# Four blocks of an FP4 layer, the scatters and the gathers of a mixture: another place in the order of a woven kernel

## The chip, the cores and the metric

The kernel runs on one core of a Trainium2 chip. A core has five engines that run side by side and wait for each other by semaphores: TensorE (PE in the profile; its weight loads are shown as PEld), VectorE (DVE), ScalarE (ACT), GpSimd (POOL) and SyncE (SP), which issues most of the transfers. Each engine takes its instructions in the order in which they stand in its own queue. The metric is the device time of one execution in microseconds, the median of the runs shown; less is better. Numbers such as L455 are lines of the kernel before the change.

## What is computed

The reference is a chain of twelve residual layers on `x`, 4 sequences of 1024 tokens with 128 features: FP4 feed-forward, softmax attention with a recurrent and a GELU part, the same FP4 feed-forward again; then twice a mixture of experts (L1) around a softmax attention, twice another mixture with a shared expert (L2) around a linear attention, twice a ternary feed-forward (L3) around another linear attention. The parts that this change touches:

```python
def fp4_quant_dequant(x):          # blocks of 16 along the last dimension
    xb = x.reshape(shape[:-1] + (shape[-1] // BLOCK, BLOCK))
    scale = jnp.maximum(jnp.max(jnp.abs(xb), axis=-1, keepdims=True) / 6.0, 1e-12)
    idx = jnp.searchsorted(_MID, jnp.abs(xb / scale))
    return (_GRID[idx] * jnp.sign(xb / scale) * scale).reshape(shape)

# layers 0 and 2:  x = x + 0.5 * _L0_ffn_ref(_layernorm(x), ...)
gate, y = fp4_linear(x, w_gate), fp4_linear(x, w_up)        # 128 -> 352
return fp4_linear(silu(gate) * y, w_down)                   # 352 -> 128

# layers 3 and 5 (6 and 8: logits softmaxed over the top two, silu(h), a shared expert)
probs = softmax(x @ gate_w.T); w, idx = top_k(probs, 2); w = w / sum(w)
for gup, dn, ce in experts:                                 # 8 experts
    g, u = split(x @ gup.T, 2); acc += ce * (silu(g) * u @ dn.T)
```

## The kernel before, in words

`x` stays in SBUF as 8 blocks of 512 tokens. `version[blk]` counts how many layers a block has been through; `need(blk, n)` lets a generator idle until the block has reached layer n.

**Woven generators.** Every layer is a Python generator that issues some instructions and yields. `run` goes through `ORDER`, a list written by hand of turns and of the layers that begin with each. A turn is a layer, or (layer, half) for the two halves (four blocks each) of a mixture. After each step of the turn, `tick` gives one step to the task at the head of each lane in `LANES`: fetch (the gathers of a half that is done), ends, front (layernorm, router, places and scatters of a mixture), alone (the shared expert), linear, ahead. The order in which instructions are issued, on all engines, follows from this weaving; a compile-time pass then orders each engine's queue by this priority and by what its estimate says is ready.

**FP4 layers** (turns 0 and 2). `l0_ffn` weaves `l0_block` over all 8 blocks, two at a time, a new one after 12 steps at the earliest. A block: layernorm; `fp4` quantises it (maximum, scale, reciprocal on DVE, a product on POOL at L447, four DVE steps L451 to L454, another product on POOL at L455); transposes; then for each of two pairs of token tiles: gate and up products (L505) into a `big` buffer of PSUM (two of them), SiLU on ACT, product on DVE (L509), `fp4` again on 128x704, transposes, down products (L521). The down products of both pairs go into one bank `out`, held over the block, and one DVE step at L527 adds half of it to `x`. That is 22 steps a block.

**Mixtures** (layers 3, 5, 6, 8). `front` takes two blocks at a time: for each, layernorm into `xn` (three buffers), transposes, router logits; then `router` and `placed` find the rows of each token at its two experts (L1099 is the cast to integer rows); then 16 scatters (L1426, an indirect transfer that POOL issues, two for each of 8 token tiles) put the normed tokens into `rows_in`. After four blocks the half's `which` (the expert of each tile) is set, and `tiles` can begin: 20 tiles of 256 rows, each with weights (L1487) and rows (L1488) loaded through SP's queue two tiles ahead, transposed (L1505), multiplied (L1546, L1555, L1532) and stored to `rows_out` (L1518). A branch at L1593 runs up to three more tiles where the data need them. `back` then gathers the results (32 gathers a half, L1625, POOL again) and adds them into `x` (L1612). Where the next half's `which` is not set when its turn comes, `run` only ticks and sets `waits_for` to the layer; `back` of that layer takes no new block meanwhile.

**Pace.** `paced` is the last DVE instruction of a few busy loops (the maxima of attention at L649, the experts' products); scatters and gathers get a semaphore wait on it (`pace`), and the second part of `layernorm` is queued behind it on DVE, so that side tasks spread over the work they stand beside.

The order around the change:

```python
ORDER = (
    ((0,), 0), ((1,), 1), (("mixtures", 2, 3), 2), ((), (3, 0)), ((4,), (3, 1)), ((5,), 4), ((), (5, 0)),
    ((6,), (5, 1)), ((), (6, 0)), ((7, 8), (6, 1)), ((), (8, 0)), ((9,), (8, 1)), (("-mixtures", 10), 9), ((11,), 11),
)
```

Of the kernel before, what the change touches and what calls it, by code (L numbers as in the profile page):

```python
# [16 lines left out]
AF = mybir.ActivationFunctionType  # L17
# [155 lines left out]
LANES = ("fetch", "ends", "front", "alone", "linear", "ahead")  # L173
# [21 lines left out]
class _Kernel:  # L195
# [6 lines left out]
    def __init__(self, ctx, tc, ins, out):  # L202
        self.tc, self.nc, self.ins, self.out = tc, tc.nc, ins, out
        self.const = ctx.enter_context(tc.tile_pool(name="const", bufs=1))
        self.small = ctx.enter_context(tc.tile_pool(name="small", bufs=4))
        self.mix = ctx.enter_context(tc.tile_pool(name="mix", bufs=2))
        self.memory = ctx.enter_context(tc.tile_pool(name="memory", bufs=1, space=bass.MemoryType.DRAM))
        self.version = [0] * NBLK
        self.paced = None
        self.easy = False  # L210
        self.waits_for = None
# [137 lines left out]
    def layernorm(self, dst, src):  # L349
# [75 lines left out]
    def fp4(self, pool, src, p, n):  # L425
# [28 lines left out]
        v.scalar_tensor_tensor(y, e, -STEP, y, ALU.mult, ALU.add)  # L454
# [28 lines left out]
    def l0_ffn(self, k):  # L483
        pool, close = self.opened("l0f", "left")
        yield from woven((self.l0_block(pool, blk, k) for blk in range(NBLK)), 2, 12)
        close()

    def l0_block(self, pool, blk, k):
# [3 lines left out]
        yield from self.layernorm(xn, self.x[blk])  # L492
# [5 lines left out]
        out = self.acc()  # L498
        for pair in range(TPB // 2):
# [13 lines left out]
            for i in range(2):  # L513
                ps = self.transposed([hq[:, i * I0 + c * C0 : i * I0 + (c + 1) * C0] for c in range(4)])
                hqT = pool.tile([C0, 4, P], F32, tag="hqT", name="hqT", bufs=4)
                nc.scalar.copy(hqT.rearrange("p c t -> p (c t)"), ps[:C0, :])
                hqTs.append(hqT)
                yield
            for i in range(2):
                for c in range(4):  # L520
                    nc.tensor.matmul(  # L521
                        out[:, bass.ts(2 * pair + i, D)], lhsT=hqTs[i][:, c, :], rhs=self.wdT[:, c, :],
                        start=c == 0, stop=c == 3,
                    )
# [95 lines left out]
    def maxima(self, pool, n, qb, causal):  # L620
# [8 lines left out]
        for t in range(TPB):  # L629
            q = qb * TPB + t  # L630
            keys = (q + 1) * P if causal else S
            for c in range(0, keys, BLK):
                w = min(keys - c, BLK)
                diag = causal and c + w == keys
                for pair in range(2):
# [7 lines left out]
                    if diag:  # L643
# [5 lines left out]
                    self.paced = nc.vector.tensor_reduce(  # L649
                        to[:, pair::2, t], ps[:, :, :w], AX.X, ALU.max, negate=True  # L650
# [585 lines left out]
    def l3_ffn(self, k):  # L1236
# [22 lines left out]
        for two in range(0, NBLK, 2):  # L1259
            hs = []  # L1260
            for blk in (two, two + 1):
# [4 lines left out]
                for c in range(NC):  # L1266
                    ps = self.big()
                    for j, m in enumerate((w1, w2)):
                        nc.tensor.matmul(ps[:, j, :], lhsT=m[:, bass.ts(c, P)], rhs=xnT, start=True, stop=True)  # L1269
                    nc.scalar.activation(h[:, c, :], ps[:, 0, :], AF.Silu, scale=scale(0, c))  # L1270
                    nc.vector.scalar_tensor_tensor(  # L1271
                        h[:, c, :], ps[:, 1, :], scale(1, c), h[:, c, :], ALU.mult, ALU.mult
# [5 lines left out]
            for i0, m in ((2, h1), (3, h2)):  # L1278
                for z in range(2):
                    h = pool.tile([P, NC, BLK], F32, tag="h", name="h", bufs=4)  # L1280
                    for pair in range(NC // 2):
# [30 lines left out]
    def run(self):  # L1312
# [47 lines left out]
class _Mixture:  # L1360
# [27 lines left out]
    def front(self, half, first, blocks):  # L1388
# [28 lines left out]
        half.todo += blocks  # L1417
        if half.todo == HALF:
# [16 lines left out]
        if half.todo == HALF:  # L1435
# [3 lines left out]
    def twice_silu(self, h, x):  # L1439

        self.k.nc.scalar.activation(h, x, AF.Tanh, scale=0.5)  # L1441
        self.k.paced = self.k.nc.vector.scalar_tensor_tensor(h, h, 1.0, x, ALU.add, ALU.mult)
# [52 lines left out]
    def tiles(self, half, behind):  # L1495
# [43 lines left out]
        def products(j, w, xT, first=None, last=None):  # L1539

            nonlocal waiting
            for c in range(0, NC, many):
# [10 lines left out]
                else:  # L1553
                    nc.scalar.activation(h, ps[:, :many, :], AF.Silu)  # L1554
                    k.paced = nc.vector.tensor_tensor(h, h, ps[:, many:, :], ALU.mult)  # L1555
# [46 lines left out]
    def back(self, half):  # L1602
# [51 lines left out]
```

## Time and profile before

| what | us |
|---|---|
| median of 3 runs | 4490.01 (4486.51 to 4496.32) |
| the profiled execution | 4454.02 |
| its span, first to last instruction | 4452.3 |
| first FP4 layer, blocks done (L527) | 71 to 223 |
| attention of layer 1, last maxima | 1091; its tail ends at 1279 |
| second FP4 layer, blocks done | 1187, 1241, 1281, 1320, 1344, 1373, 1413, 1435 |
| scatters of blocks 0 and 1, of 2 and 3, of 4 to 7 | 1292 to 1316, 1372 to 1394, 1451 to 1525 |
| tiles of (3, 0), (3, 1) | 1442 to 1568, 1568 to 1753 |
| attention of layer 4 | to about 2661 |
| tiles of (5, 0), (5, 1) | 2661 to 2785, 2785 to 3002 |
| tiles of (6, 0), (6, 1) | 3009 to 3165, 3175 to 3354 |
| tiles of (8, 0), (8, 1) | 3417 to 3585, 3598 to 3711 |
| last layers (L3, linear attention, L3) | 3711 to 4452 |

The borders of the stages come from the times of a line's instructions. In the busy table a stretch is followed by the busy time of each engine with the number of its instructions, the granted TensorE clock as a share of full speed, the share of DMA engines busy and the gigabytes per second. In a timeline, a line is a run of like instructions: start, length, engine, line, operation, what it writes and reads, how many, and in brackets the idle time of the engine before it and what ended it. In a list of waits, the three numbers are the sum, the times and the longest.

### The profile page before, as it was taken

What the parts mean: (1) busy time and instruction counts of PE and PEld (TensorE: products, weight loads), DVE (VectorE), ACT (ScalarE), POOL (GpSimd) and SP (SyncE); (2) the same over time, 40 slices, a digit from 0 to 9 for tenths busy, and PEclk for the clock granted to TensorE, in tenths of its full rate; (3) what the DMA queues carried; (4) which work ended last, traced back from release to release, by engine and by line L of the source; (5) the groups of instructions that cost most, each with busy time, mean ns of one, the idle gap of its engine ahead of it and who ended that gap; (6) DMA issues with size and microseconds to landing.
All of it is one profiled execution on the core that took longest, in us unless ns stands there. A gap on an engine that the chain in (4) does not pass through costs nothing. (4 is left out here: it accounts for less than half of the span.)

```text
span 4452.3 us, 59962 instructions
## 1 busy us (share of the span) xinstructions
PE 3783.8 (85%) x21360; PEld 1963.3 (44%) x21360; DVE 2665.9 (60%) x6035; ACT 1704.7 (38%) x3066; POOL 1024.5 (23%) x1334
## 2 busy tenths in 40 slices
PE   4659999999665978899989999887795978999999
PEld 3513333333344865222222338665563654444444
DVE  8657878785777446788888854535574653223201
ACT  1216454545222222566656662222231322333322
POOL 5313323222244231202020101324324142000000
PEclk8759899999876999999999999998897989999999
DMA  2011101000001553101010005434422352000000
GB/s 103 1 47 46 37 21 39 21 29 7 1 10 37 184 166 101 44 28 39 28 64 27 30 15 188 134 117 130 136 90 72 110 155 75 1 0 0 5 5 10
DMA packets 140628, 261.74 MB, mean 59 GB/s; under 512 B 25803, under 2 KB 90187, under 8 KB 139683
## 3 DMA queue, kind: packets, MB, share of 16 engines
q1 hardware_dynamic: 123939, 224.23, 15.6%
q0 software_dynamic: 16384, 33.59, 2.5%
q8 instruction: 174, 2.85, 0.3%
q14 instruction: 131, 1.07, 0.1%
HBM read 197.31 MB, written 60.42 MB: 58 GB/s over the span
## 5 line engine op out<-in xcount | busy, mean ns | idle before, releaser
L827 ACT ACTIVATE es<-sc 128x512 f32<-128x512 f32 (+3 forms) x1792 | 892.2, 549 | 576.3 <-PE sc L820 572.8
L649 DVE TENSOR_REDUCE part<-big 128x2 f32<-128x1024 f32 (+3 forms) x768 | 877.0, 1154 | 178.2 <-PE big L639 119.5
L742 PE MATMUL acc<-es,va 128*32 128x256 f32 (+2 forms) x6144 | 566.9, 411 | 4.1 <-POOL es L830 3.4
L1546 PE MATMUL big<-xT,w 128*128 128x256 f32 x1968 | 514.3, 402 | 24.1 <-DMA w<-in_l2f_w 9.8
L639 PE MATMUL big<-most 64*128 64x512 bf16 (+3 forms) x1792 | 385.3, 368 | 93.0 <-DMA most<-pieces 58.0
L1285 PE MATMUL big<-h,l3f_w 128*128 128x512 f32 x1024 | 446.6, 593 | 5.3 <-DVE h L1271 2.3
L1546 PEld LDWEIGHTS big<-xT,w 128*128 128x128 f32 x1968 | 387.1, 202 | 103.5 <-issue 35.4
L815 PE MATMUL sc<-most 64*128 64x512 bf16 (+3 forms) x1792 | 394.8, 371 | 24.8 <-ACT es L827 11.6
L361 POOL TENSOR_TENSOR ln_rs<-ln_ve,neg_half 128x4 f32<-128x4 f32 x120 | 125.8, 1049 | 1158.1 <-DVE ln_ve L360 1133.7
L1625 POOL DMA_INDIRECT y<-rows_out,rows x256 | 246.9, 965 | 564.4 <-DVE h L1555 155.2
L820 PE MATMUL sc<-last 64*128 64x512 bf16 (+3 forms) x1792 | 376.5, 365 | 0.0
L1532 PE MATMUL acc<-h,w 128*128 128x256 f32 x1304 | 342.8, 394 | 24.1 <-DVE h L1555 16.0
L1426 POOL DMA_INDIRECT rows_in<-xn,rows x256 | 249.8, 976 | 473.7 <-DVE p_to L1114 91.2
L1285 PEld LDWEIGHTS big<-h,l3f_w 128*128 128x128 f32 x1024 | 191.9, 190 | 239.1 <-issue 230.1
L830 POOL TENSOR_SCALAR_AFFINE_SELECT es<-es 128x128 f32<-128x128 f32 x512 | 171.3, 345 | 526.5 <-ACT es L827 521.2
L1532 PEld LDWEIGHTS acc<-h,w 128*128 128x128 f32 x1304 | 241.1, 197 | 67.8 <-DVE h L1555 23.7
L742 PEld LDWEIGHTS acc<-es,va 128*32 128x32 f32 x6144 | 135.7, 109 | 297.7 <-issue 242.5
L815 PEld LDWEIGHTS <-most 64*128 64x128 bf16 x1792 | 94.3, 93 | 376.2 <-issue 353.1
L1554 ACT ACTIVATE h<-big 128x512 f32<-128x512 f32 x166 | 99.1, 597 | 402.5 <-PE big L1546 394.7
L1441 ACT ACTIVATE h<-big 128x1024 f32<-128x1024 f32 x112 | 114.4, 1024 | 328.2 <-PE big L1546 238.3
L639 PEld LDWEIGHTS <-most 64*128 64x128 bf16 x1792 | 110.8, 95 | 236.1 <-issue 119.2
L1612 DVE SCALAR_TENSOR_TENSOR x<-y,weights,x 128x128 f32<-128x128 f32 x256 | 90.9, 361 | 207.0 <-DMA y<-rows_out,rows 206.0
(291 smaller groups left out, 5195.4 us busy)
## 6 DMA issues: line engine op xcount, KB each, us to landing
w<-in_l1f_w SPq DMA_DIRECT2D x86, 768.0 KB
w<-in_l2f_w SPq DMA_DIRECT2D x84, 512.0 KB
most<-pieces SPq DMA_DIRECT2D x512, 48.0 KB
xr<-rows_in SPq DMA_DIRECT2D x170, 128.0 KB
rows_out<-yr SPq DMA_DIRECT2D x163, 128.0 KB
pieces<-pieces SPq DMA_DIRECT2D x32, 384.0 KB
most<-pieces SPq DMA_DIRECT2D x256, 32.0 KB
rows_in<-zero SPq DMA_DIRECT2D x4, 1472.0 KB
```

The costliest lines, as they stand in the source:

```text
L639: nc.tensor.matmul(ps[:, j, :w], lhsT=of[:, 0, bass.ts(q, P)], rhs=of[:, 1, c : c + w], start=True, stop=not diag,)
L649: self.paced = nc.vector.tensor_reduce(to[:, pair::2, t], ps[:, :, :w], AX.X, ALU.max, negate=True)
L742: nc.tensor.matmul(out[0][32 * i : 32 * i + 32, lo:hi], lhsT=self.vas[b % 2][:, kc, (4 * g + i) * (HD + 1) :][:, :32], rhs=es[i][:, lo:hi] ...
L815: nc.tensor.matmul(ps[:, off:], lhsT=of[:, 1, keys], rhs=of[:, 0, queries], start=True, stop=False)
L820: nc.tensor.matmul(ps[:, off:], lhsT=of[:, 1 + pair, keys], rhs=of[:, 0, queries], start=False, stop=True,)
L827: nc.scalar.activation(es[i][:, off:], ps[:, off:], AF.Exp, scale=ISQ)
L830: nc.gpsimd.affine_select(out=block, in_=block, compare_op=ALU.is_ge, fill=0.0, base=0, pattern=[[1, P]], channel_multiplier=-1,)
L1285: nc.tensor.matmul(ps[:, j, :], lhsT=m[:, i * FF + (2 * pair + j) * P : i * FF + (2 * pair + j + 1) * P], rhs=hs[z][:, i, :], start=i == 0 ...
L1426: put = nc.gpsimd.indirect_dma_start(out=k.rows_in[half.h][:, :], out_offset=bass.IndirectOffsetOnAxis(ap=at, axis=0), in_=xns[t // TPB][: ...
L1532: nc.tensor.matmul(outs[j][:, :TT], lhsT=w[:, low + c * D :][:, :D], rhs=h, start=c == 0, stop=c == NC - 1)
L1546: nc.tensor.matmul(ps[:, i, :], lhsT=w[:, bass.ts(col, P)], rhs=xT, start=True, stop=True)
L1625: got = nc.gpsimd.indirect_dma_start(out=y, out_offset=None, in_=k.rows_out[half.h][:, :], in_offset=bass.IndirectOffsetOnAxis(ap=self.row ...
```

## The change

Layer 2 handles only its first four blocks in its turn and puts the other four, as one generator, into a new lane `ffn`; the main loop goes on to (3, 0) meanwhile. `l0_block` adds each pair of token tiles into `x` by itself, from a bank that it asks for only then (19 steps a block; layer 0 too). Scatters are a generator `put` in a new lane `puts`; `front` goes on without them, but holds at most three `xn` tiles (`held`). `waits_for` is now the half that the main loop waits for, and the gathers of the other half, whatever their layer, stop before each gather until that half begins. FP4's last DVE step, L3's products and L3's GELU now set the pace too; `pacer` is what transfers wait for, `paced` what layernorms are queued behind. FP4's own layernorm is not queued behind anything.

```diff
-LANES = ("fetch", "ends", "front", "alone", "linear", "ahead")
+LANES = ("fetch", "ends", "puts", "front", "alone", "linear", "ffn", "ahead")
...
-        with nullcontext() if self.paced is before else self.tc.issue_after(self.paced.ins):
+        with nullcontext() if in_turn or self.paced is before else self.tc.issue_after(self.paced.ins):
...
-        if self.paced is not None:
-            self.tc.add_manual_dep(transfer.ins, self.paced.ins.name, SYNC, reason="pace")
+        if self.pacer is not None:
+            self.tc.add_manual_dep(transfer.ins, self.pacer.ins.name, SYNC, reason="pace")
+
+    def passed(self, instruction):
+
+        self.paced = self.pacer = instruction
...
-        v.scalar_tensor_tensor(y, e, -STEP, y, ALU.mult, ALU.add)
+        self.passed(v.scalar_tensor_tensor(y, e, -STEP, y, ALU.mult, ALU.add))
...
-        yield from woven((self.l0_block(pool, blk, k) for blk in range(NBLK)), 2, 12)
-        close()
+
+        def blocks(first, last):
+            yield from woven((self.l0_block(pool, blk, k) for blk in range(first, last)), 2, 12)
+            if last == NBLK:
+                close()
+
+        if k == 0:
+            yield from blocks(0, NBLK)
+        else:
+            yield from blocks(0, HALF)
+            self.beside("ffn", blocks(HALF, NBLK))
...
-        yield from self.layernorm(xn, self.x[blk])
+        yield from self.layernorm(xn, self.x[blk], True)
...
-        out = self.acc()
+        x = self.x[blk].rearrange("p t d -> p (t d)")
         for pair in range(TPB // 2):
...
+            out = self.acc()
             for i in range(2):
                 for c in range(4):
                     nc.tensor.matmul(
-                        out[:, bass.ts(2 * pair + i, D)], lhsT=hqTs[i][:, c, :], rhs=self.wdT[:, c, :],
+                        out[:, bass.ts(i, D)], lhsT=hqTs[i][:, c, :], rhs=self.wdT[:, c, :],
                         start=c == 0, stop=c == 3,
                     )
-                yield
-        x = self.x[blk].rearrange("p t d -> p (t d)")
-        nc.vector.scalar_tensor_tensor(x, out, 0.5, x, ALU.mult, ALU.add)
-        self.version[blk] += 1
-        yield
+            these = x[:, bass.ts(pair, 2 * D)]
+            nc.vector.scalar_tensor_tensor(these, out[:, : 2 * D], 0.5, these, ALU.mult, ALU.add)
+            if pair == TPB // 2 - 1:
+                self.version[blk] += 1
+            yield
...
-                            nc.scalar.activation(h[:, c, :], ps[:, j, :], AF.Gelu, scale=scale(i0, c))
+                            self.pacer = nc.scalar.activation(h[:, c, :], ps[:, j, :], AF.Gelu, scale=scale(i0, c))
...
-                self.waits_for = turn[0]
+                self.waits_for = turn[1]
...
             yield from k.need(blk, self.number)
+            while k.held == max(TOGETHER) + 1:
+                yield
+            k.held += 1
...
-        for t in range(n):
+        k.beside("puts", self.put(half, first * TPB, xns, which))
+
+    def put(self, half, first, xns, which):
+
+        k, nc = self.k, self.k.nc
+        for t in range(len(xns) * TPB):
             for i in range(2):
-                at = self.rows[:, i, first * TPB + t : first * TPB + t + 1]
+                at = self.rows[:, i, first + t : first + t + 1]
                 put = nc.gpsimd.indirect_dma_start(
...
+            if t % TPB == TPB - 1:
+                k.held -= 1
+        if which is not None:
             k.apart(half.puts)
             half.which = which
...
-            while k.waits_for == self.number:
-                yield
             for t in range(blk * TPB, (blk + 1) * TPB):
                 for i in range(2):
+                    while k.waits_for == 1 - half.h:
+                        yield
                     y = k.mix.tile([P, D], F32, tag="y", name="y", bufs=4 * TPB)
```

The steps at L649, L1442 and L1555 that were assigned to `paced` are now passed to `passed`, and so is L1271. L1599, which sets `paced` back to what it was ahead of the branch, stays as it is.

More of the change, by code (lines that the diff above doesn't have):

```diff
@@ L209, in __init__ @@
         self.paced = None
+        self.pacer = None
         self.easy = False
+        self.held = 0
         self.waits_for = None
@@ L346, in clear_rows, with layernorm @@
                 )
-    def layernorm(self, dst, src):
+    def layernorm(self, dst, src, in_turn=False):
         nc = self.nc
@@ L648, in maxima @@
                     to = mx if one else part[:, c // BLK]
-                    self.paced = nc.vector.tensor_reduce(
-                        to[:, pair::2, t], ps[:, :, :w], AX.X, ALU.max, negate=True
+                    self.passed(
+                        nc.vector.tensor_reduce(
+                            to[:, pair::2, t], ps[:, :, :w], AX.X, ALU.max, negate=True
+                        )
                     )
@@ L1270, in l3_ffn @@
                     nc.scalar.activation(h[:, c, :], ps[:, 0, :], AF.Silu, scale=scale(0, c))
-                    nc.vector.scalar_tensor_tensor(
-                        h[:, c, :], ps[:, 1, :], scale(1, c), h[:, c, :], ALU.mult, ALU.mult
+                    self.passed(
+                        nc.vector.scalar_tensor_tensor(
+                            h[:, c, :], ps[:, 1, :], scale(1, c), h[:, c, :], ALU.mult, ALU.mult
+                        )
                     )
@@ L1417, in front @@
         half.todo += blocks
+        which = None
         if half.todo == HALF:
@@ L1434, in front @@
                     yield
-        if half.todo == HALF:
+            if t % TPB == TPB - 1:
+                k.held -= 1
+        if which is not None:
             k.apart(half.puts)
@@ L1441, in twice_silu @@
         self.k.nc.scalar.activation(h, x, AF.Tanh, scale=0.5)
-        self.k.paced = self.k.nc.vector.scalar_tensor_tensor(h, h, 1.0, x, ALU.add, ALU.mult)
+        self.k.passed(self.k.nc.vector.scalar_tensor_tensor(h, h, 1.0, x, ALU.add, ALU.mult))
     def alone(self, blk):
@@ L1554, in products @@
                     nc.scalar.activation(h, ps[:, :many, :], AF.Silu)
-                    k.paced = nc.vector.tensor_tensor(h, h, ps[:, many:, :], ALU.mult)
+                    k.passed(nc.vector.tensor_tensor(h, h, ps[:, many:, :], ALU.mult))
                 next(leaving, None)
```

## The prediction

> **What bounds the kernel now.** I read the page first, then the busy table cut at the stage borders, then the waits of PE and the timelines at the borders that hold a hole.
>
> ```profile
> span 4452.3 us, 59962 instructions
> PE 3783.8 (85%) x21360; PEld 1963.3 (44%) x21360; DVE 2665.9 (60%) x6035; ACT 1704.7 (38%) x3066; POOL 1024.5 (23%) x1334
> ...
> PE   4659999999665978899989999887795978999999
> ...
> PEclk8759899999876999999999999998897989999999
> ```
>
> PE is the busiest engine, and over most slices it is full, so time is won only where PE waits: slices 11 to 13 (1110 to 1440 us: the second FP4 layer), and slice 31 (3340 to 3450 us). There the granted clock falls too. The busy table (columns: stretch, length, PE, PEld, DVE, ACT, POOL, clock, DMA share, GB/s):
>
> ```profile
> 1110.00:1320.00 210.00, 144.10 (x608) 83.50 (x604) 155.07 (x431) 57.72 (x100) 77.99 (x73) 0.80 0.02 6
> 1320.00:1397.00 77.00, 35.95 (x171) 28.54 (x172) 54.92 (x176) 13.24 (x23) 38.85 (x34) 0.69 0.14 47
> 1397.00:1442.00 45.00, 29.88 (x147) 24.42 (x145) 32.40 (x107) 9.65 (x17) 15.91 (x14) 0.73 0.02 5
> 1442.00:1568.00 126.00, 122.38 (x599) 104.32 (x599) 60.59 (x185) 35.05 (x68) 37.88 (x40) 0.98 0.54 178
> 1568.00:1753.00 185.00, 150.13 (x652) 111.03 (x652) 97.45 (x200) 38.70 (x71) 36.00 (x36) 0.91 0.44 146
> ...
> 3165.00:3175.00 10.00, 0.76 (x5) 0.46 (x4) 1.12 (x3) 0.00 (x0) 4.84 (x5) 0.64 0.30 93
> ...
> 3354.00:3417.00 63.00, 12.97 (x39) 6.30 (x39) 24.52 (x123) 3.44 (x5) 41.90 (x43) 0.62 0.23 73
> 3417.00:3585.00 168.00, 152.13 (x695) 110.02 (x696) 112.27 (x349) 55.41 (x90) 36.65 (x38) 0.97 0.35 111
> 3585.00:3598.00 13.00, 3.54 (x17) 2.38 (x15) 2.73 (x5) 0.29 (x2) 7.44 (x8) 0.74 0.38 126
> ```
>
> The fourth row is (3, 0), the first half of the mixture behind the FP4 layer: PE 122 of 126 us busy. The rows above it are the FP4 layer, which runs on latency: no engine is full. What PE waits for there is the last step of a quantisation, on POOL:
>
> ```profile
> PE tr L377 <- POOL fp_y L455: 89.0, 16, 21.8
> ```
>
> The first instruction of (3, 0) comes without any wait just before it, behind FP4's and the router's matmuls in PE's own order:
>
> ```profile
> 1432.19 3.20 PE L521 MATMUL acc<-wdT,hqT 88*128 88x128 f32 x16
> ...
> 1442.14 1.11 PE L377 MATMUL tr<-ident,xr 128*128 128x128 f32 x4
> ```
>
> Its rows were there long before: the last scatter of its half ran at 1393 us. So (3, 0) could have begun at about 1400 us. The second hole, before (8, 0), is a wait for rows:
>
> ```profile
> 3387.30 0.95 POOL L1625 DMA_INDIRECT y<-rows_out,rows  x1 [0.30 <-issue]
> 3388.55 1.00 POOL L1426 DMA_INDIRECT rows_in<-xn,rows  x1 [0.30 <-issue]
> ...
> 3417.03 1.09 PE L377 MATMUL tr<-ident,xr 128*128 128x128 f32 x4 [14.45 <-DMA xr<-rows_in]
> ```
>
> The places of these scatters (L1099, the cast of the rows) were known at 3376 us in DVE's timeline; POOL was still in 22 gathers of the half before (3356 to 3388), and the scatters had to queue behind them.
>
> **The change, part by part.** A step of the woven generators I call a tick. A tile of an expert takes four, a half of 20 tiles 80; (8, 0) took 168 us, so a tick there is 2.1 us.
>
> *Four FP4 blocks beside (3, 0).* Blocks 4 to 7 issue no DMA, but each puts 68 matmuls and transposes on PE, 7 instructions on POOL (3 at L447, 3 at L455, one at L361, 1.1 to 1.6 us each: 10 us) and some 20 us on DVE (its rows' means added up). By ticks, blocks 0 to 3 end at tick 55, the front of blocks 2 and 3 and its 16 scatters at about 84; until then main waits and blocks 4, 5 and a bit of 6 run as before. So only about two blocks come beside the tiles. Gain: (3, 0) starts at 1400, not 1442: -42. Given back: the 29.9 us of PE work of 1397 to 1442 now stand inside a stage where PE is full: at the clock of that stage 29.9 x 0.73 / 0.98 = 22, at its old speed 30; I take 25. New stalls, because FP4's products hold the two `big` buffers and its DVE work stands between a tile's matmuls and its `h`: at least nothing, at most the difference between a tile of the crowded (3, 1), 185 / 20 = 9.2 us, and one of (3, 0), 126 / 20 = 6.3 us, over the 6 tiles that the two blocks last: 18. I take 4, since DVE and ACT of (3, 0) are half idle. Sum -42 + 25 + 4 = -13; ends: -28 (22 given back, no stall, and block 3 done 8 us sooner since block 4 starts behind it: blocks end 22 us apart in the first FP4 layer, 22 to 54 in the second) and +6 (30 and 18).
>
> The scatters of (3, 1), 32 in 74 us there, get FP4's POOL work ahead of them in that queue, some 20 us; POOL has 88 of 126 us free, and (3, 1) needs its last rows at 1568 where the scatters ended at 1525. Cost nothing; without that room they would end 20 us later, at 1545, still ahead of 1568.
>
> Quantisation beside scatters has a row: of the scatters at 1372 to 1394, two beside FP4's DVE steps at L451 and L452 took 1.28 and 1.26 us, the others about 0.96. At 0.3 us each, 32 scatters lose 10 us of a POOL with 88 free: nothing on the path. The Trainium skill gives a reason that speaks against this place: DMA: Bandwidth & Descriptors, section SWDGE vs HWDGE vs iDMA, says that the descriptor rings which GpSimd writes for its DMAs lie in memory that VectorE locks GpSimd out of in its two-port mode. By that rule an estimate is a whole L452 (0.52 us) for each scatter, 17 us, and the sum stays the same.
>
> *Accumulators by pair.* Sixteen blocks have two residual steps of 128x256 for one of 128x512. One is 0.68 us; the nearest of 128x256 out of PSUM (L1517) is 0.42. So 2 x 0.42 - 0.68 = +0.16 us of DVE a block; 1.3 us in the first FP4 layer, where DVE is 114 of 163 us busy, hidden in the second. The output bank is free sooner, but PE's wait there (6.3 us a block) is for L455, not for a bank. Take +1, ends -8 and +8 (a microsecond a block either way).
>
> *Scatters in a lane of their own.* The front of the next two blocks no longer stands behind the 16 scatters of the two before; only its second block still does behind the first eight, for there are three `xn` buffers. (6, 1): its blocks were ready at 3080, eight scatters had gone by 3098, that block's layernorm came at 3099, but its logits at 3127, the rows at 3151, the last scatter at 3170, and PE stood from 3165 to 3175. Issued up to 16 ticks (34 us) earlier, the same work ranks before the tiles' that it stood behind; with half of that the hole goes, and a 3.6 us wait for weights behind it, as the tile loop itself now fetches for the next half: -12 (ends 0 and -14). (6, 0): its rows come sooner too, but the tiles inside the branch at L1593 ran until 3002; only the late fetch goes (7.1 us wait for `xr`): -5 (ends 0 and -9). Such a fetch waits for the scatters on SP's queue, ahead of later stores of `yr` (L1518); with the scatters done sooner that wait is short.
>
> *(8, 0) and (8, 1).* The layernorms of blocks 2 and 3 waited until 3335 for scatters; the first eight were through at 3329, so 6 us sooner, rows at 3370. No gathers ahead of the scatters: 16 x 1.27 = 20, to 3390, and the loads 5 us: tile at 3395, not 3417: -22. But the 32 gathers held back are those of (6, 1), and (8, 1) depends on them through linear attention. They ran from 3356 to 3437; now they start at 3395, one a tick: 32 x 2.1 = 67, to 3462, 25 us later. Against that, (8, 1)'s own front no longer waits for 16 scatters (ready 3505, transposed 3535 and 3548; now some 8 us after it is ready): -30. So (8, 1) starts at about 3593 instead of 3598. Of all that -5 is left, and I take -3, as the eight scatters still stand before its last block: ends -25 (gathers no later) and +30 (25 later, and nothing won by the front).
>
> *Pace by more instructions.* FP4's and L3's steps now pace scatters and layernorms; beside the L3 layer the 32 gathers of (8, 1) ran unpaced at 3713 to 3753 and will spread. The blocks they feed are used some 20 ticks later. L1599 sets back `paced` alone, so a transfer issued next waits for the branch; before (8, 0) the rows at 3370 come after its end at 3354 anyway. 0, ends -5 and +5 (the 5 us of PE waits at 3729 to 3739, gone or doubled).
>
> Sum: -13 + 1 - 12 - 5 - 3 = -32 us on the profiled execution's 4454.0 us (span 4452.3), that is 4422. The median of the runs shown is 4490.0, 36 above that execution; I keep the difference: **4458 us**.
>
> **Rivals.** *Nothing won at (3, 0):* the two blocks give back all 42 us, as PE work and stalls (30 + 12), and only the later borders gain: 1 - 12 - 5 - 3 = -19, 4471. For it: PE at 122 of 126. Against: the clock of 0.73 in what is moved.
>
> *It does not do what it says:* the wait for half 0 is so long in ticks that the four blocks are used up in it, or the order drawn up at compile time keeps their earlier matmuls first, and the hole at 3165 is set by its data: 4487, within 0.2% of before (what a measurement can tell). For it: 30 of the 56 ticks of the side task pass in that wait.
>
> *Slower: the held gathers.* Place: (6, 1)'s gathers behind the start of (8, 0). If they go as in (5, 1), 32 in 90 us, they end at 3485, 48 us later than now, and if nothing is won by the front behind them (8, 1) starts at 3646; the tiles begun earlier in (8, 0) only wait there. +48 less the other 29 is +19: 4509. It decides from 29 us of delay at (8, 1). For it: (8, 1) already waits 8.8 us for its rows. Against: its front has 30 us to give.
>
> **How the numbers follow.** Forecast (4420 to 4469) 0.48; nothing at (3, 0) 0.15; not done 0.15; slower 0.22. The range: the forecast with its two widest terms at their good ends (-15 and -22) is 4458 - 37 = 4421, less 9 for the first layer, and up to the slower rival: 4412 to 4509. Faster 0.63, same 0.15, slower 0.22.
>
> **What would show it.** Right: L1505 of (3, 0) starts near 1400 us with L521 among its first matmuls; (3, 0) ends before 1568; no hole at (6, 1); scatters ahead of gathers before (8, 0). Wrong: tiles of (3, 0) above 9 us each; a hole of over 60 us before (8, 1); a changed first FP4 layer (22 us a block).

## The result and the profile after

The changed kernel took 4472.6 us (median of 6 runs, 4465.6 to 4480.8), the kernel before 4492.4 beside it (6 runs): a ratio of 0.9948 [0.9929, 0.9967], 20 us faster. The forecast was 4458 in a range of 4412 to 4509. In the profiled execution, though, there is no gain at all: 4465.6 us against 4454.0. The experiments had to settle which of the two is the change. Line numbers have moved: L455 is now L461, L521 is L539, L1271 is L1292, L1426 is L1457, L1593 is L1626, L1612 is L1645, L1625 is L1658.

The page of the changed kernel (engine totals, then slices of PE and of its granted clock):

```profile
span 4463.9 us, 60027 instructions
PE 3775.5 (85%) x21360; PEld 1954.9 (44%) x21360; DVE 2667.4 (60%) x6051; ACT 1705.6 (38%) x3066; POOL 1028.3 (23%) x1334
...
PE   4659899999756887899989999897786969999999
...
PEclk8759999999876899999999999999898989999999
```

The totals are those of before within 0.5%. The weak slices around 1300 us are still there, and a second weak one has come after the one at 3400. The busy table of the changed kernel, cut at the same borders as before (stretch, length, PE, PEld, DVE, ACT, POOL, clock, DMA share, GB/s):

```profile
1320.00:1408.00 88.00, 41.45 (x156) 30.24 (x154) 50.50 (x174) 12.31 (x21) 40.97 (x39) 0.60 0.14 48
1408.00:1522.00 114.00, 87.89 (x420) 72.55 (x419) 69.64 (x204) 26.85 (x50) 40.59 (x36) 0.83 0.22 75
1522.00:1601.00 79.00, 73.92 (x359) 62.92 (x358) 34.76 (x113) 20.83 (x40) 21.66 (x23) 0.98 0.52 176
1601.00:1786.00 185.00, 147.75 (x642) 109.56 (x639) 96.59 (x198) 38.27 (x70) 36.02 (x36) 0.93 0.43 146
...
3395.00:3423.00 28.00, 0.92 (x4) 0.58 (x4) 3.35 (x25) 0.16 (x1) 16.29 (x17) 0.56 0.36 120
3423.00:3590.00 167.00, 143.35 (x630) 102.97 (x629) 112.09 (x346) 50.47 (x83) 49.41 (x50) 0.92 0.36 115
3590.00:3637.00 47.00, 18.96 (x85) 13.02 (x83) 16.16 (x67) 5.31 (x8) 21.10 (x22) 0.75 0.29 93
```

(3, 0) is now the second and third row. It begins at 1408 instead of 1442, but takes 193 us instead of 126: while FP4 blocks run beside it (to 1522), PE is busy 88 of 114 us at a clock of 0.83. Its eight tiles of that stretch take some 14 us each (114 / 8); those after it, at 0.98, about 6. The last row, the stretch ahead of (8, 1), has PE idle for 28 of 47 us; the same row of before was 13 us long. The timeline of PE in the changed kernel at the three borders (start, length, what is written and read, idle time before it and what ended it):

```profile
1407.60 0.66 PE L379 MATMUL tr<-ident,xr 128*128 128x128 f32 x2 [4.08 <-DMA xr<-rows_in]
...
1417.94 1.73 PE L539 MATMUL acc<-wdT,hqT 88*128 88x128 f32 x14
...
3422.09 1.43 PE L379 MATMUL tr<-ident,xr 128*128 128x128 f32 x5 [27.39 <-DMA xr<-rows_in]
...
3636.58 1.39 PE L379 MATMUL tr<-ident,xr 128*128 128x128 f32 x5 [27.00 <-DMA xr<-rows_in]
```

The first two lines show the side task as it was meant: FP4's down products (L539) stand among the first matmuls of (3, 0). The last two are the same wait for rows, 27 us before each half of layer 8; before the change these were 14 and 9 us.

### The profile page after: what moved, and what is told of

Read it like the earlier page. It is cut to its first block, busy times and chain, and to the rows that moved or that the text cites. A ratio compares the mean times of both kernels' runs of the same rounds, so it can differ in the third digit from the quotient of the medians.

```text
span 4463.9 us, 60027 instructions
## 1 busy us (share of the span) xinstructions
PE 3775.5 (85%) x21360; PEld 1954.9 (44%) x21360; DVE 2667.4 (60%) x6051; ACT 1705.6 (38%) x3066; POOL 1028.3 (23%) x1334
## 5 line engine op out<-in xcount | busy, mean ns | idle before, releaser
L1579 PE MATMUL big<-xT,w 128*128 128x256 f32 x1968 | 508.6, 398 | 33.8 <-ACT xT L1538 10.2
L1307 PE MATMUL big<-h,l3f_w 128*128 128x512 f32 x1024 | 446.8, 593 | 4.0 <-ACT h L1314 1.5
L1579 PEld LDWEIGHTS big<-xT,w 128*128 128x128 f32 x1968 | 382.1, 200 | 112.3 <-issue 35.4
L1658 POOL DMA_INDIRECT y<-rows_out,rows x256 | 247.2, 965 | 625.4 <-DVE part L668 122.5
L1457 POOL DMA_INDIRECT rows_in<-xn,rows x256 | 249.5, 975 | 418.0 <-DVE part L668 125.7
L1307 PEld LDWEIGHTS big<-h,l3f_w 128*128 128x128 f32 x1024 | 191.8, 190 | 237.8 <-issue 229.7
L1645 DVE SCALAR_TENSOR_TENSOR x<-y,weights,x 128x128 f32<-128x128 f32 x256 | 89.3, 354 | 289.9 <-DMA y<-rows_out,rows 260.9
L835 PEld LDWEIGHTS <-most 64*128 64x128 bf16 x1792 | 94.1, 93 | 375.5 <-issue 354.2
L379 PE MATMUL tr<-ident,fp_y 128*88 128x128 f32 (+1 forms) x324 | 71.4, 390 | 167.5 <-POOL fp_y L461 167.5
```

The costliest lines, as they stand in the source:

```text
L835: nc.tensor.matmul(ps[:, off:], lhsT=of[:, 1, keys], rhs=of[:, 0, queries], start=True, stop=False)
L1307: nc.tensor.matmul(ps[:, j, :], lhsT=m[:, i * FF + (2 * pair + j) * P : i * FF + (2 * pair + j + 1) * P], rhs=hs[z][:, i, :], start=i == 0 ...
L1457: put = nc.gpsimd.indirect_dma_start(out=k.rows_in[half.h][:, :], out_offset=bass.IndirectOffsetOnAxis(ap=at, axis=0), in_=xns[t // TPB][: ...
L1579: nc.tensor.matmul(ps[:, i, :], lhsT=w[:, bass.ts(col, P)], rhs=xT, start=True, stop=True)
L1658: got = nc.gpsimd.indirect_dma_start(out=y, out_offset=None, in_=k.rows_out[half.h][:, :], in_offset=bass.IndirectOffsetOnAxis(ap=self.row ...
```

## The experiments

Twelve runs were made, four on each of three chips, here A, B and C, beside runs of the kernel before on the same chip. Differences in us are the kernel's median less that of before.

| kernel | chip, before there | median, us | less before | ratio [95%] |
|---|---|---|---|---|
| before, again | A, 4447.4 | 4450.3 | +3 | 1.0005 [0.9988, 1.0022] |
| one output bank a block | A | 4438.2 | -9 | 0.9974 [0.9959, 0.9988] |
| no side task | A | 4459.3 | +12 | 1.0028 [1.0015, 1.0041] |
| old hold | A | 4451.6 | +4 | 1.0017 [1.0003, 1.0032] |
| changed, again | B, 4498.0 | 4484.8 | -13 | 0.9967 [0.9954, 0.9980] |
| old pace | B | 4505.3 | +7 | 1.0015 [1.0005, 1.0025] |
| no lane for scatters | B | 4494.9 | -3 | 0.9996 [0.9983, 1.0008] |
| one bank, no side task, old hold | B | 4484.4 | -14 | 0.9965 [0.9952, 0.9978] |
| before, a third time | C, 4448.2 | 4446.1 | -2 | 0.9992 [0.9979, 1.0006] |
| changed, a third time | C | 4460.9 | +13 | 1.0026 [1.0011, 1.0040] |
| late lane | C | 4413.1 | -35 | 0.9915 [0.9898, 0.9933] |
| late lane and side task | C | 4410.8 | -37 | 0.9913 [0.9895, 0.9931] |

A and C are alike in level, B is 50 us slower with the same program, and the change is worth 13 us there and costs 13 on C. So the 36 us between the profiled execution of before and its timed runs most likely go with the chip: where before takes 4447 and 4448 us, its profiled executions span 4451.5 and 4446.8. On which chips the first profile and the first timed runs were made is not on record, so this is argued, not shown. The kernels are compared on one chip, or on A and C, unless it is said otherwise.

**The kernel before, again (A), the changed kernel again (B), both a third time (C).** Unedited.

> The kernel before, unchanged, with a second profile. The first profiled execution (4454 us) lies 36 us below the median of the timed ones (4490), and the changed kernel's profile is 12 us longer than it while its median is 20 us shorter. Theory: that execution was a lucky one, and this profile is near 4485, the 30 us spread over the stages at a lower granted clock. Rival: the 36 us sit in one stage, such as the second FP4 layer or the start of the last feed-forward layers, where the change then gains more than the two profiles show.

> The changed kernel, unchanged, with a second profile, beside the kernel before on the same chip. By the two first profiles it should be 12 us slower than the kernel before; by the first comparison of their timed runs it is 20 us faster (0.9948). Theory: the loss is real where the chip's level is near 4450 us and this ratio is 1.002 to 1.004. Rival: the gain is real everywhere, the ratio is 0.995 again and the first profile of the changed kernel was a slow execution.

> The kernel before once more, with a profile, on the same chip as the changed one in the next run: so far their profiles come from chips 1 per cent apart (the kernel before took 4447 us on one and 4498 on another). Theory: stage by stage the difference is the same as on the other chip (first FP4 layer +13, (3, 0) and (3, 1) +20, start of L3 -20), and what made the first pair of profiles differ by +12 is the two chips. Rival: there is a stage that only the slower chip stretches in the kernel before.

> The changed kernel on the same chip as the run above. By the second comparison 0.9967 of the kernel before: 10 to 20 us less. If its gain depends on the chip, the ratio is above 0.999 on a chip where the kernel before takes about 4450 us.

The pair on chip C is the only one with both traces from the same chip. Stage by stage, from the starts of the tiles:

| stage (us, chip C) | before | changed | difference | forecast |
|---|---|---|---|---|
| first FP4 layer, to its last block | 221 | 236 | +15 | +1 |
| from there to the end of (3, 0) | 1345 | 1371 | +26 | -13 |
| (3, 1), attention of layer 4, (5, 0) | 1221 | 1215 | -6 | 0 |
| (5, 1) | 218 | 209 | -9 | -5 |
| (6, 0) and the hole behind it | 166 | 165 | -1 | -12 |
| (6, 1), (8, 0) and their holes | 423 | 435 | +12 | -3 |
| (8, 1), last layers | 853 | 827 | -26 | 0 |
| sum | 4447 | 4458 | +11 | -32 |

The last row of stages is -4 for (8, 1) and -22 for the last layers. The tiles of a half are taken to start with its first transposes; counted from its first product (L1546 before, L1579 changed), the four rows from (5, 1) on are -4, -6, +9 and -23, as PE waits some 4 us for weights between the two at some borders and not at others. The changed kernel on B against C: +33 in the profiled executions, spread over stages ((3, 1) with the attention of layer 4 +10, (5, 1) +11, (6, 0) +7). DMA packets take as long on both (those of 6144 bytes 297 and 298 ns). No trace of the kernel before exists from a chip of B's level; why it loses more there than the changed kernel does stays open.

**One output bank a block.** The changed kernel, with the block's `out` and its one residual step as before:

```diff
+        out = self.acc()
         for pair in range(TPB // 2):
...
-            out = self.acc()
...
-                        out[:, bass.ts(i, D)], lhsT=hqTs[i][:, c, :], rhs=self.wdT[:, c, :],
+                        out[:, bass.ts(2 * pair + i, D)], lhsT=hqTs[i][:, c, :], rhs=self.wdT[:, c, :],
...
-            these = x[:, bass.ts(pair, 2 * D)]
...
+                yield
+        x = self.x[blk].rearrange("p t d -> p (t d)")
+        nc.vector.scalar_tensor_tensor(x, out, 0.5, x, ALU.mult, ALU.add)
```

> The changed kernel, but each FP4 block keeps one output bank for both pairs and adds to x once (22 steps a block again). Theory: the accumulators by pair cost the first FP4 layer its 13 us (last block at 236 instead of 223 us), because 19 steps at 12 apart leave less of two blocks side by side; here the last block of layer 0 is done at 223 again and the kernel is 10 to 16 us faster than the changed one. Rival: the 13 us come from the new pace by FP4's last DVE step; then nothing moves.

It is 0.9974 on A where the changed kernel is 1.0026 on C, another chip of the same level: some 23 us. The first FP4 layer ends at 217 us. In all fourteen traces it ends at 217 to 223 with one bank and at 235 to 239 with a bank a pair; the rival, FP4's pace, is out, as without that (old pace, below) it still ends at 238. The waits of PE in that layer, 110 to 210 us (sum in us, times, longest), in the changed kernel and then in this one:

```profile
PE tr L379 <- POOL fp_y L461: 35.0, 4, 9.4
```

```profile
PE tr L379 <- POOL fp_y L461: 33.4, 7, 7.3
```

The sum is alike (28.1 us in 6 waits in the kernel before); the waits are longer and fewer with pairs, which does not account for the 18 us. A block has 19 steps there instead of 22, with the next one still let in after 12, so two blocks overlap otherwise. Which of the two parts of the edit does it, banks or steps, was not tried apart, and how stays open.

**No side task.** The changed kernel with all eight blocks in the layer's own turn:

```diff
-        if k == 0:
-            yield from blocks(0, NBLK)
-        else:
-            yield from blocks(0, HALF)
-            self.beside("ffn", blocks(HALF, NBLK))
+        yield from blocks(0, NBLK)
```

> The changed kernel, but all eight blocks of the second FP4 layer in its own turn. Theory: beside the tiles of (3, 0) the side task costs more than it wins (tiles 14 us each while two FP4 blocks run, 6 alone), so without it (3, 1) starts some 10 to 20 us earlier after the start of (3, 0) is corrected for, and the kernel is 10 to 20 us faster. Rival: FP4 has to be done somewhere, and the side task is worth its place: 10 to 30 us slower.

1.0028 on A, as the changed kernel has 1.0026 on C: in the changed kernel the side task is worth nothing that can be measured. (3, 0) takes 128 us, so the tiles are themselves again; but it starts 144 us after the fourth FP4 block, where before it started after 122, though blocks 4 to 7 are back in the layer's own turn. Something else of the change costs there. It is not the bank or the hold: with these undone too (one bank, no side task, old hold, below) it is 147 us, and 122 again only with the lane of layer 3 and FP4's pace undone as well (late lane).

**Old hold.** Gathers held back by layer, ahead of a block, as before:

```diff
-                self.waits_for = turn[1]
+                self.waits_for = turn[0]
...
+            while k.waits_for == self.number:
+                yield
...
-                    while k.waits_for == 1 - half.h:
-                        yield
```

> The changed kernel, but gathers are held back as before, by layer and by block. Theory: the hold wins 20 us at (8, 0) and loses them at (8, 1), so (8, 0) starts some 20 us later, (8, 1) some 20 to 30 us earlier, and the kernel is within 10 us of the changed one. Rival: the hold is a net gain of 20 us or more.

From the start of (6, 1) to that of (8, 1) it takes 423 us, as before, against the changed kernel's 435. The profiled execution is 8 us shorter, but in the timed ratios (1.0017 and 1.0026, overlapping intervals) the price of the hold is not resolved.

**Old pace.** FP4's last DVE step, L3's products and L3's GELUs set no pace:

```diff
-        self.passed(v.scalar_tensor_tensor(y, e, -STEP, y, ALU.mult, ALU.add))
+        v.scalar_tensor_tensor(y, e, -STEP, y, ALU.mult, ALU.add)
...
-                            self.pacer = nc.scalar.activation(h[:, c, :], ps[:, j, :], AF.Gelu, scale=scale(i0, c))
+                            nc.scalar.activation(h[:, c, :], ps[:, j, :], AF.Gelu, scale=scale(i0, c))
```

> The changed kernel, but FP4's last DVE step and the L3 layer's products and GELUs set no pace. Theory: the pace by the L3 layer spreads the 32 gathers of (8, 1) and is what wins some 20 us at the start of the first L3 layer (its first 32 matmuls take 16 us instead of 35), so this run is 15 to 25 us slower from there on; at the second FP4 layer nothing much moves. Rival: the start of L3 is faster for another reason (fewer gathers left), and this run is within 5 us of the changed one.

20 us slower than the changed kernel on the same chip, intervals apart. The last layers take 745 us instead of 719, and L3's first 32 matmuls 33 us instead of 16; the stages of the second FP4 layer do not move (1373 against 1372). So the gain is the pace in L3. The edit also undoes the place of L3's layernorms behind its products; the two were not tried apart. How it acts is seen in the traces of chip C. The kernel before, DVE's timeline just behind the last mixture, and its waits from 3704 to 3745 us:

```profile
3719.27 0.36 DVE L1612 SCALAR_TENSOR_TENSOR x<-y,weights,x 128x128 f32<-128x128 f32 x1 [0.71 <-DMA y<-rows_out,rows]
3720.69 0.35 DVE L1612 SCALAR_TENSOR_TENSOR x<-y,weights,x 128x128 f32<-128x128 f32 x1 [1.07 <-DMA y<-rows_out,rows]
3721.86 0.35 DVE L1612 SCALAR_TENSOR_TENSOR x<-y,weights,x 128x128 f32<-128x128 f32 x1 [0.82 <-DMA y<-rows_out,rows]
3722.13 0.74 DVE L1271 SCALAR_TENSOR_TENSOR h<-big,l3f_s,h 128x512 f32<-128x512 f32 x1
```

```profile
DVE x L1612 <- DMA y<-rows_out,rows: 26.1, 24, 5.8
...
PE big L1269 <- DVE h L1271: 12.4, 5, 5.9
```

The changed kernel, its waits from 3737 to 3765 us:

```profile
DVE x L1645 <- DMA y<-rows_out,rows: 9.3, 8, 2.2
...
PE big L1289 <- DVE h L1292: 0.5, 2, 0.3
```

The gathers were unpaced and landed some 1.3 us apart; the additions that use them stood at the head of DVE's queue and waited for each, and L3's products (L1271) stood between them. PE waited for those: 12.4 us in 5 waits for L1271 in the same stretch. With the pace there are 8 waits for gathers in that stretch, and no wait of PE for L1292 there is above 0.5 us. The waits for gathers are not gone: the gathers now last until 3915 us, and up to there DVE waits 26 times, 99.2 us in all. But most of this falls beside the later products of L3 (L1307), and PE waits for L1292 only 2.6 us in 4 waits from 3737 to 3925.

**No lane for scatters.** The front of a mixture issues its scatters itself:

```diff
-        k.beside("puts", self.put(half, first * TPB, xns, which))
+        yield from self.put(half, first * TPB, xns, which)
```

> The changed kernel, but the scatters are issued inside the front again. Theory: the lane of their own brings the rows of (6, 1) and (8, 0) earlier, so both holes grow by 5 to 15 us and the kernel is 10 to 25 us slower. Rival: three xn buffers hold the front back all the same, and it is within 5 us.

By the timed runs the lane is worth 10 us on chip B, the intervals only just apart. Its profile shows two signs in that: without the lane (5, 1) takes 228 us instead of 220 and (6, 0) 180 instead of 172, so the lane wins 16 there; but from the first FP4 layer to the end of (3, 0) it takes 1355 instead of 1372, so the lane loses 17 there. These two profiled executions as a whole stand the other way round than the timed medians (span 4483.4 without the lane, 4491.0 with it, the longest of its five runs), so the 10 us rest on the timed runs alone.

**One bank, no side task, old hold.** The three edits above in one kernel, meant as the best of them.

> The changed kernel with three parts undone together: one output bank per FP4 block, all eight blocks in their own turn, gathers held by layer and block; the lane for scatters and the wider pace stay. Theory: the three losses add up (19 + 7 + 14 us on the profiles of the single ones), so this is 30 to 40 us faster than the changed kernel and 20 to 30 us faster than the one before. Rival: they are not independent, as a start of the tiles that comes later also hides the order of the gathers: 10 to 20 us.

No gain over the changed kernel on the same chip (0.9965 and 0.9967). With the lane and FP4's pace left in, the stretch from the first FP4 layer to the end of (3, 0) is the longest of all kernels, 1387 us.

**Late lane; late lane and side task.** One bank, the old hold, no pace from FP4 (L3's stays), and the lane only from layer 5 on; the first without, the second with the side task:

```diff
-        k.beside("puts", self.put(half, first * TPB, xns, which))
+        if self.number == 3:
+            yield from self.put(half, first * TPB, xns, which)
+        else:
+            k.beside("puts", self.put(half, first * TPB, xns, which))
```

> The FP4 layers and layer 3 as before (one output bank, eight blocks in their own turn, scatters inside the front, no pace by FP4, old hold of the gathers); kept are the lane for scatters from layer 5 on and the pace by the L3 layer. Theory: these two are the whole gain (13 us by the lane, 20 by the pace), and what the FP4 parts do is loss: 25 to 35 us faster than the kernel before. Rival: the lane is worth little without the new hold: 15 to 22 us.

> The run above plus the side task alone: blocks 4 to 7 of the second FP4 layer beside (3, 0). It gives the price of the side task by itself. Theory: (3, 0) starts 40 us earlier and its tiles take 14 us each while FP4 runs, so (3, 1) starts 5 to 20 us later than without it and the kernel is that much slower. Rival: without FP4's pace on the scatters and layernorms the two fit, and it is 5 to 20 us faster.

Both beat both kernels: 0.9915 and 0.9913. They can't be told from each other, so even here the side task is worth 2 us, within the interval. Its stage is a different one, though. The busy tables of (3, 0), while FP4 runs and after it, in the changed kernel on chip C:

```profile
1413.00:1525.00 112.00, 87.95 (x400) 73.42 (x401) 65.56 (x194) 25.36 (x48) 36.15 (x31) 0.80 0.21 66
1525.00:1607.00 82.00, 78.49 (x378) 66.98 (x376) 38.12 (x121) 21.96 (x43) 26.10 (x27) 0.96 0.57 183
```

and in the late lane with the side task:

```profile
1401.00:1475.00 74.00, 63.14 (x327) 52.19 (x326) 44.73 (x137) 20.27 (x39) 21.69 (x19) 0.92 0.25 82
1475.00:1559.00 84.00, 82.25 (x417) 70.20 (x417) 41.94 (x136) 23.88 (x46) 30.21 (x32) 1.00 0.59 193
```

158 us instead of 194. PE stands 13 us instead of 28, and it is busy 145 us instead of 166: 34 matmuls fewer, and a clock of 0.92 and 1.00 instead of 0.80 and 0.96. PE's waits for L461 in the first stretch are 8.5 us in 2 instead of 20.4 in 5. One of those five, in the timelines of DVE, POOL and PE of the changed kernel on chip C:

```profile
1477.08 0.53 DVE L457 TENSOR_SCALAR fp_e<-fp_y 128x704 int32<-128x704 int32 x1 [1.56 <-POOL fp_y L453]
1477.52 0.68 DVE L1588 TENSOR_TENSOR h<-h,big 128x512 f32<-128x512 f32 x1
1478.12 1.14 DVE L369 TENSOR_SCALAR xn<-x,ln_mv,ln_rs 128x128 f32<-128x128 f32 x4
1479.18 0.51 DVE L458 TENSOR_SCALAR fp_e<-fp_e 128x704 f32<-128x704 f32 x1
...
1481.35 0.88 DVE L460 SCALAR_TENSOR_TENSOR fp_y<-fp_e,fp_y 128x704 f32<-128x704 f32 x1
...
1481.70 1.36 POOL L1457 DMA_INDIRECT rows_in<-xn,rows  x1 [1.89 <-DVE h L1588]
1483.36 0.96 POOL L1457 DMA_INDIRECT rows_in<-xn,rows  x1 [0.30 <-issue]
1484.35 1.39 POOL L461 TENSOR_TENSOR fp_y<-fp_y,fp_scale 128x704 f32<-128x704 f32 x1
...
1485.80 1.08 PE L379 MATMUL tr<-ident,fp_y 128*88 128x128 f32 x4 [6.15 <-POOL fp_y L461]
1486.67 0.63 PE L379 MATMUL tr<-ident,yo 128*128 128x128 f32 x2
```

FP4's four DVE steps take 2.8 us (L457 to L460), but with the tiles' `h` and a layernorm between them they end 5.2 us after they began, at 1482.2. On POOL two scatters then go first, so L461 starts at 1484.4. PE stands 6.15 us at the transposes of `fp_y`, the head of its queue, with the tiles' own matmuls behind them. That is one wait in full. The one before 1513 us, of 5.83 us, is alike: two scatters stand ahead of L461. The other three (4.45, 2.98 and 0.97 us) have no scatter between; there L461 starts as soon as L460 is done, or within 0.2 us of it.

From the first FP4 layer to the end of (3, 0) the changed kernel took 1366, 1371 and 1372 us in its three traces, and 1362 with the old hold, which has no part in this stretch, as the first gather comes after it. So differences of 10 us between two such traces are not resolved. Undone one at a time, the lane takes 17 us from it on B and FP4's pace nothing (-1); what the bank a pair and the side task take (1360 and 1367 without them, on A) lies within that spread. With all of these but the side task undone it is 1336, and with that undone too 1345, as in the kernel before (1345 to 1349 in three traces): there, in one trace against four, the side task by itself makes this stretch 9 us shorter.

The late lane's lead over before in the profiles, 4409.3 against 4446.8, lies elsewhere: the last layers take 720 us instead of 743, (5, 1) 210 instead of 218, (3, 1) with the attention of layer 4 1090 instead of 1097. What it keeps of the change is the pace in L3, the lane from layer 5 on, the limit on `xn` tiles, and FP4's layernorm outside the pace. Which of these wins the 14 us outside the last layers was not tried apart.

## Why the prediction was right, and where it was wrong

The direction was right where it was first measured (a level of 4492, near that of B) and on chip B, wrong on chip C; 4472.6 lies in the range, 15 us over the point. But the sum behind it is not confirmed. It was -32 on the profiled execution, which came out at +12 (+11 on chip C); the 36 us kept between that execution and the median became 7. That second step was an assumption about runs which most likely is one about chips, and its error of -29 covers most of the first one's +44: that the point came so near is luck. By its steps, on chip C unless it is said otherwise:

- **Four blocks beside (3, 0): -13, found +26 with the parts of lane and bank.** The start was nearly right: 1408 and 1413 for a forecast 1400, 28 to 35 us earlier than before. The stage was not. It was to be 126 + 25 + 4 = 155 us and is 194. Of the 39, 19 are PE's busy time (166 against 122 + 25, at a clock of 0.80 beside FP4 where the forecast took that of a full stage) and 20 are idle time (28 against 4 + 4). Two steps failed. The first is "until then main waits and blocks 4, 5 and a bit of 6 run as before". Block 4 was done at 1388 us and block 5 at 1424, 11 us behind the start of the tiles, where before block 5 was done at 1372 and block 6 at 1412: more of FP4 was left for the stage. On chip B these two are done at 1390 and 1426 with the lane (tiles from 1413) and at 1367 and 1403 without it (tiles from 1417); how the lane holds them up was not followed. In the late lane with the side task they are done at 1350 and 1390, ahead of the tiles at 1400, and there the forecast nearly holds: (3, 0) takes 158 us and the stretch is 9 us shorter than without the side task. The second is "I take 4, since DVE and ACT of (3, 0) are half idle": with (3, 0)'s own 4 taken off, the new idle time is 24 us, and 9 in the late lane. As the wait of 6.15 us shows, an engine half idle on average still puts a chain of dependent steps behind its other work at each link, and PE, in order, waits at the end of the chain. The upper end of that term, from a tile of 9.2 us, was too low as well: the tiles took 14. This is what the forecast had put down as its sign of being wrong.
- **Scatters of (3, 1) beside FP4: "Cost nothing".** It looked at when the scatters end, not at what stands behind them on POOL. In two of the five waits of PE above, two scatters went ahead of L461. The 17 us by which the stretch is shorter without the lane on chip B are mostly another matter: the 23 us of blocks 4 and 5 are lost ahead of the first of these scatters (at 1480 us with the lane, 1476 without).
- **Accumulators by pair: +1, found +15,** beyond its end of +8. The step counted DVE instructions; when the bank is asked for, and three steps fewer in a block that is woven with another, were left out. A first FP4 layer that changes from its 22 us a block was named as a sign; it now has 24.
- **Scatters' lane: -17 in (5, 1) and (6, 0), found -10** (-16 by the undone lane on chip B). The hole before (6, 1) is still there: a wait of 4.7 us in the changed kernel (7.3 in its first profile), now put down to SP's queue at the branch (L1626), and 3.4 for weights behind it.
- **Held gathers: -3, found +12** (+9 from the first products). The first half was right: (6, 1) with its hole is 21 us shorter for a forecast 22, and the gathers go from 3412 to 3476, 64 us for a forecast 67. The failed step is the -30 for the front of (8, 1): from the last gather to the start of (8, 1) it took 162 us before and takes 155. Its scatters go from first to last in 73 us instead of 87, but the first comes 78 us after the last gather instead of 71. So the slower rival's mechanism came, at a delay of 19 us (last gather 280 us after the start of (6, 1), 261 before) where the forecast had 25 and that rival 48, with 7 us won in the front instead of 30: 21 of gain, 33 of loss.
- **Pace: 0, found -22,** the largest gain of the change and outside its ends of -5 and +5. The working saw 5 us of PE's waits at 3729 to 3739. The trace of before has, from 3711 to 3752 us, 26.6 us of DVE's waits for gathers in 24 and 13.8 us of PE's for L1271 in 4, on the path of the main stream; the term took only part of these.
- **Scatters beside two-port steps of DVE:** The mean of all 256 scatters is 975 ns in the changed kernel and 976 before. The 32 of (3, 1), which now run beside FP4's steps, take 1007 ns on average where they took 967, three of them more than 1.2 us: 1.3 us in all, where the forecast put 10. The estimate of 17 by the rule of the Trainium skill (DMA: Bandwidth & Descriptors, section SWDGE vs HWDGE vs iDMA) is not reached either. In the row that the forecast read, the second slow scatter (1386.39 us) stood beside L453 and L454, not L452.

"Not done" is out: the order changed as told. "Nothing won at (3, 0)" describes the side task within the changed kernel, where its removal leaves the time as it was (1.0028 on A, 1.0026 with it on C); the later borders that were to gain in that case gave 20 us in the last layers instead.

## What to carry to other kernels

A side task made of long chains of short dependent steps costs the main stream at each link that comes back to an in-order queue, so cost it by the chain and by who stands behind its last wait, not by the idle share of the engines, and ask how much of it is left when the main stream starts: what came of the same side task depended on what else was moved with it. When a queue gets new work, ask who queues behind it: here two scatters of about 1 us went ahead of a product that PE was waiting for. Look, too, for instructions that wait for transfers at the head of an engine's queue and hold up all behind them; pacing those transfers was the largest gain here, some 20 us, and it did not shorten the waits but moved them to where PE had other work.

## What was not expected of the chip

The same program takes 4447 us on two chips and 4498 on another, and the ratio of two programs differs between them (1.0026 [1.0011, 1.0040] and 0.9967 [0.9954, 0.9980]): a comparison of less than 1% holds for the chip that it was made on. In the rows of (3, 0) above the mean granted clock is lower where PE stands idle for more of the time: 0.80 in the 112 us in which PE was busy 88, 0.92 in the 74 in which it was busy 63, 1.00 in the 84 in which it was busy 82. The matmuls of (3, 0), with those of FP4 beside them, took 166 us of PE in the changed kernel and 145 in the late lane with the side task, for 778 and 744 records.
